# New time offsets for the steps of a two-layer graph attention kernel ordered by a timetable

## The chip, the cores and the metric

The kernel runs on one core of one Trainium2 chip. The metric is the device time of one execution in microseconds (us), the median of several. One profiled execution of the kernel is read as well: every time below that names an instruction comes from it, counted from the first instruction of the span. The engines are PE (TensorE, matmuls and transposes), DVE (VectorE), ACT (ScalarE), POOL (GpSimd) and SP (SyncE, which here only issues DMAs). "L1131" is line 1131 of the kernel before; the change makes the file 6 lines shorter, so the same line of the kernel after is L1125.

## What is computed

The input x has 16 batches of 1024 nodes with 256 features, adj is one 1024 x 1024 adjacency matrix for all batches. Two layers, both in fp32:

```python
# layer 0
h   = relu(layernorm(x))
r   = relu(h @ mlp1_w + mlp1_b)                   # 1024 x 512
o   = elu(gat(r, None, W_fc, a_fc)) + r           # dense attention, slope 0.2
r   = relu(o @ mlp2_w + mlp2_b)                   # 1024 x 256
o   = elu(gat(r, adj, W_hand, a_hand)) + r        # masked attention, slope 0.2
x   = x + relu(o)
# layer 1
h   = relu(layernorm(x)) @ W
x   = x + relu(softmax(where(adj == 0, -1e9, leaky_relu(f1 + f2, 0.01))) @ h)

def gat(inp, mask, W, a):
    h  = inp @ W
    e  = leaky_relu((h @ a[:F])[:, :, None] + (h @ a[F:])[:, None, :], slope)
    return elu(softmax(e, masked) @ h)
```

## The kernel before

**Stages of a batch.** A batch passes through these stages, each a small class whose methods are the steps; node tiles have 128 rows, the two halves h of a batch have four tiles each.

- Norm and BlockNorm: statistics (L571, L572), the root on POOL (L576, L577; for BlockNorm L613 to L616), centring on DVE (L581), then the turned copy: transposes nt on PE (L591) with a copy on ACT (L595), or, from batch 3 on, transposes in 32-blocks on DVE (L627) and moves by SP's DMAs (L637).
- Dense, the first attention. mlp1 (PE L805, ACT L808) gives resT; sums_of (DVE L819, L821, POOL L823, L825) forms sums of its rows, from which `step` (PE L834) makes the values h and adds them into hnat (ACT L856, DVE L866, L874). As this attention has no mask, its rows are sorted by their score instead of multiplied out: `highest` (PE extdps, DVE topd L911), `rank` for each of 8 tiles (DVE L926, L928, L930, L933), `scatter` of the rows to DRAM (POOL L940), `sign` (ACT L963) and `count` (DVE L969) for each node's place k, `read_sorted` (SP L984), running sums over the sorted rows (DVE L1012 to L1027), `write_table` (SP L1019) and `carry` (PE, ACT, SP L1041) into two tables in DRAM, a fine and a coarse one. `gather` (POOL L1051, indirect DMA) then fetches for every node tile a fine row, and adds the coarse row to it: 8 fine and 8 coarse gathers a batch, into four tiles got_b_h_i. `share` (DVE L1063 to L1066) makes the denominators den; `mean` is part on ACT (L1072) and hp on DVE (L1075). Batch 0 alone makes its first half by plain products instead: weights (L1095), od (PE L1103) and `product_mean` (hpd, L1110 to L1114).
- merge, four for each half: transposes hpT of the four hp on PE (L1121), three ACT operations (L1123 to L1125), then merge_end: e on DVE (L1131) and the add into resT on POOL (L1132). After it mlp2 (m2, PE L1139) with ACT's oT (L1142).
- Gnn0 and Gnn1, the two masked attentions: project (pa or pb on PE L669, copied by ACT L671), extremes (DVE L676, L677, PE extpsa or extpsb L546, DVE topa or topb L686), vectors, a row of the vector through DRAM (L551 to L554, L707), scale (ACT L716), the weights of eight tiles (atta, attb on DVE L722), product (oa, ob on PE L732), finish, combine, update and store.

PSUM has four buffers for mm (h, od, m, oa, ob), two for tr (nt, hpT, extps) and one for bc.

**What sets the order.** There is no loop order to read: every step is put into one table with a time, in units of about a microsecond, by `at`:

```python
def at(name, lo, hi, steps):
    for i, step in enumerate(steps):
        key = part + name
        moved = SHIFT.get(key, ())
        k = turn[key] = turn.get(key, -1) + 1
        when = lo + (hi - lo) * i / len(steps) + (moved[k] if k < len(moved) else 0.0)
        table.append((when, len(table), step))
```

`part` is "start " for the opening (batches 0 to 2 before the first period), "first " for batch 0's period, "mid " for the periods 1 to 12 and "end " for the last three. A period is 142 units in the table. Several batches are in flight in one period: in the period of batch b the masked attentions of b and b-1 run, the sorted sums, gathers, merges and mlp2 of b+1, and the norm, mlp1 and values of b+2 and b+3. SHIFT (L31 on) is a dict with an offset for each step of a name; steps beyond the tuple's length have offset 0. At the end the table is sorted by time, and the steps are issued in that order. The order on PE, DVE, ACT and SP is then fixed to it, and POOL's is fixed by added dependencies, except among scatters (L940):

```python
with tc.manual_schedule(engines={engine.PE, engine.DVE, engine.Activation, engine.SP}):
    for _, _, step in sorted(table, key=lambda entry: entry[:2]):
        step()
```

The times have no other effect: no engine waits for a time, only for its operands, for buffers, and for the instruction before it in its own order. So SHIFT decides who stands behind whom.

Of the kernel before, what the change touches and what calls it, by code (L numbers as in the profile page):

```python
# [31 lines left out]
    "end dense_begin1": (-5.56,),  # L32
    "end dense_begin2": (-5.2, -5.18,),
    "end dense_begin3": (-5.5,),
    "end dense_begin4": (0, -2.9, -8.1, -9.4, -12.6, -15.2, -16.2, -19.3,),
    "end dense_begin5": (-21.7, -21.7,),
    "end dense_begin6": (-28.9, -18.2, -16.02, -20.3, -24.3, -25.3,),
    "end dense_begin7": (-25.8,),
    "end dense_end1": (-12.1, -3.3,),
    "end dense_end2": (-12, -6.6, -10.6, -11.3, -2.6, -2.6, -2.6, -2.6,),  # L40
    "end dense_rows1": (-6.1, -4.2, -29.3, -23.4, -23.5, -14.8, -10.8, -13.4, -8.4, -6.6, -33.8,
        -30.8, -40.4, -34.9, -28.2, -31.9,),
    "end dense_rows2": (-13.4, -11.4, -1.5, -1.9, -10.7, -11.5, -21.9, -22.3, -13.6, -14.6, -8.3,
        -8.7, -6.5, 0, -24.5, -28, -23.8, -25.6, -18.6, -19.58,),
    "end dense_rows3": (-7.9, -2.4,),
    "end dense_rows4": (-24.8,),
    "end dense_sums10": (-42.6,),
    "end dense_sums11": (6.1,),
    "end dense_sums12": (-7.3,),
    "end dense_sums2": (-5.3, -3.9, -10.1, -10.2, -15.7, -13.2, -13.4, -12.6,),  # L50
    "end dense_sums3": (-8.7, -6,),
    "end dense_sums4": (-8.91, -10.158, -11.4, -12.648, -5.3, -5.3, -2.5, -3.4,),
    "end dense_sums7": (-3.2, -3.8, -4.6, -6, -6.8, -6.1, -7.7, -5.3,),
    "end dense_sums9": (-2.3,),
    "end early_gathers1": (-4.3, -4.29,),
    "end early_gathers2": (0, 0.002,),
    "end early_gathers3": (11.9, 19.3, 5, 13.2,),
    "end early_gathers4": (-8.55, -6.9, -1.7, -3.7, 9.2, 11.4, 4.7, 4.7,),
    "end first_mlp1": (-23.2, -18.7, -5.2, -8.6,),
    "end first_mlp2": (-52.8, -63.5, -84.1, -44.8,),  # L60
    "end masked_first1": (-16,),
    "end masked_first10": (-11.3, -10.91, -13.14, -13.74, -7.2, -8.1, -2.8, -3.4,),
    "end masked_first11": (-11.7, -11.1, -10.8, -11.45, -6.5, -7.2, -2.5, -3.1,),
    "end masked_first12": (-1.4, -1,),
    "end masked_first13": (-14.1, -13.6, -10.5, -11.76, -1, 1.3, 0, -1,),
    "end masked_first14": (-11.7, -8.6, -10.2, -11.95, 4.5, 4.5, 0, -0.5,),
    "end masked_first15": (-11.7,),
    "end masked_first16": (-0.3,),
    "end masked_first2": (-13,),
    "end masked_first3": (-14.3,),  # L70
    "end masked_first4": (-16.8,),
    "end masked_first5": (-18.4, -16.1, -16.5, -15.8, -13, -12.9, -16.3, -16,),
    "end masked_first6": (-24.6,),
    "end masked_first7": (-21.5, -16, -7.4, -22.8,),
    "end masked_first8": (-23.8, -6.8, -20.1, -18.4,),
    "end masked_first9": (-9.2, -10.06, -10.8, -10, -9.2, -9.8, -10.4, -10.9, -11.2, -11.63, -12.5,
        -10.8, -11.66, -11.6, -12, -12.7, -10.8, -10.8, -10.8, -10.8, -10.8, -10.8, -10.8, -10.8,
        -7.5, -6.9, -7, -6.9, -6, -5.3, -3.7, -3.7, -15.8, -10.7, -9.4, -7.5, -6.2, -4.3, -4.1,
        -2.2,),
    "end masked_second1": (-2.34, -3.204, -4.068, -4.932, -5.796, -6.6, -4.2, -4.2, -4.2, -4.2,  # L80
        -4.2, -4.2, -2, -2, -2, -2, -2, -2, -3.1, -2.34, -2.76, -3.18, -0.5, -0.9, -1.1, -1.1,
        -1.1, -1.1, -1.1, -1.1, -25.3, -24.3, -22.2, -18.2, -11, -10.97,),
    "end masked_second2": (-6.7, -6.7, -2.7, -2.7, -1.9, -1.9, -1, -1, -0.9, -0.9, -10.91,),
    "end masked_second3": (-7.2, -3.7, -2.81, -3.5, -1.5, -1.2, -0.7, -1.3,),
    "end masked_second4": (-4.6, -3.8, -3.7, -4.5,),
    "end masked_second5": (21.3, 31.4, 28.4, 30.2, 28.1, 19.5,),
    "end masked_second6": (0, 19.2,),
    "end merges1": (-5.9, -8.2, -2.29, -3.5, 0, -3, 3.3, 0.3,),
    "end merges2": (-3.2, -3, -3.96, -5.8, 3.5, 0.71, 2.7,),
    "end scatters1": (1.2, -0.6, -12.1, -8.7, -19.5, -21.3, -19.1, -24.8,),  # L90
    "end second_mlp1": (-8.9, 2.6, 1, 1.3,),
    "end second_mlp2": (-21.6, -13.8, -13.6, -22.6, -19.2, -20.4, -17.2, -22.2,),
    "end second_mlp3": (-17.9,),
    "end second_norm1": (-6.4, -5.3, -7.9, -8.2, -6, -7, -7.8, -8.6,),
    "end second_norm2": (-9.2,),
    "end second_norm3": (-9.3,),
    "end second_norm4": (-10.15,),
    "end second_norm5": (-10.3, -7.4, -7.5, -6.6, -7.5, -7.2, -5.41, -6.5,),
    "end second_norm6": (-12.3,),
    "end second_norm7": (-18.8,),  # L100
    "end second_norm8": (-32.2, -30.7, -31.2, 0, 0, 0, 0, -29.5,),
    "end turn_at1": (-8.8, -11.7, -12.1, -13.5, -1.46, -1.7, -2.1, -2.5,),
    "end turn_at2": (-8.1, -5.4, -7.8, -4.8, -2.6, -2.6, -2.6, -2.6,),
    "end weights a": (-18.1, -18.6, -19.1, -15.1, -10.2, -13, -9.7, -21.1, -8, -6.4, -11, -7.04,
        -7.85, -13.6, -10.9, -27.8, -9.7, -32.2, -10.2, -11.1, -11.4, -11.5, -15.1, -17.8, -11.6,
        -6.63, -6.7, -8.2, -6.9, -17.2, -6.7, -9.2, -11, -11.36, -10, -9.1, -11.3, -13.5, -4.7,
        -5.3,),
    "end weights b": (-9.3, -9.7, -9.5, -7.1, -8.6, -8.5, -4.1, -4.9, -5.8, -5.8, -5.8, -5.8, -5.8,
        -5.8, -5.8, -5.8, -8.8, -3.35, -2.8, -18.9, 0, -3, -12.5, -7.3, -1.5, -7.7, -2.7, 0, 0,
        -7.2, 0, 0, -7.4, 0, 0, 0, 1.8, 0, 0, 2, -25.9, -24.5, -22.9, -17.3, -10.4, -9.6, -12.8,  # L110
        -12.4,),
    "first dense_begin1": (-1.35,),
    "first dense_begin2": (-2,),
    "first dense_begin3": (-2.9,),
    "first dense_begin4": (-1.3, 2.4, 6.7, 0, 0, 0, -6.9, -11.7,),
    "first dense_begin5": (-20.3, -20.3,),
    "first dense_begin6": (-23.1, -28.8, -12.3, -26.6, -22.4, -21.7,),
    "first dense_end1": (-4.1, -4.3,),
    "first dense_end2": (-1.2, -4.1, -4.7, -3.8, 0.3, 0.3, 0.3, 0.3,),
    "first dense_rows1": (-13.9, -13.3, -20.1, -19.4, -21.8, -21.8, -17.1, -20.4, 0, -2.6, -25.3,  # L120
        -21.95, -28.5, -20.1, -23.2, -18,),
    "first dense_rows2": (-19.7, -20.3, -15.7, -12.5, -15.4, -20.8, -13.9, -13.9, -16.7, -18.5,
        -12.2, -13.43, 0, 0, -20.6, -15.8, -17.4, -11.7, -3.9, -12.2,),
    "first dense_rows3": (-19.01, -1.4,),
    "first dense_rows4": (-19.1,),
    "first first_mlp1": (-12.3, -10.8, -1.9, 15.9,),
    "first first_mlp2": (-2.8, -4.1, -22.3, -8.8,),
    "first first_norm3": (-38.92, -24.5, -24.1, -40.98, -32.7, -33.9, -31.3, -32,),
    "first first_norm4": (-24.9,),
    "first first_norm5": (-39.1, -39, -38.9, -37.7, -34.72, -45, -23.7, -22.7,),  # L130
    "first first_norm6": (-36.3, -36.2, -37.4, -36.4, -26.8, -26.8, -26.8, -26.8,),
    "first first_norm7": (-2.8, 0, 0, 6.3,),
    "first gathers1": (0, 6.1, 0, 3.75, -11.2, -6.4, -8.3,),
    "first gathers2": (1.4, 5.6, 0, 0, -4, 0, -20.8,),
    "first masked_first1": (-10.6,),
    "first masked_first10": (-9.64, -10.1, -9.2, -11.2, -2.8, -2, -3.8, -4.4,),
    "first masked_first11": (-9.6, -8.6, -7.44, -8.05, -1.4, -2, -4.99, -5.597,),
    "first masked_first13": (-9.6, -5.4, -11.4, -12.04, -5.36, -5.3, -8.5, -9.1,),
    "first masked_first14": (-6.4, -3.9, -10.2, -13, -5.3, -0.7, -8.1, -8.4,),
    "first masked_first15": (-13.3,),  # L140
    "first masked_first16": (-8.1,),
    "first masked_first4": (-12,),
    "first masked_first5": (-7.5, -7.5, -7.5, -7.5, -7.5, -7.5, -7.5, -7.5,),
    "first masked_first6": (-185.7,),
    "first masked_first8": (0, 0, 0, 13.1,),
    "first masked_first9": (-8.3, -9.1, -9.7, -10.3, -10.5, -11.2, -8.2, -8.9, -11.7, -11.7, -11.7,
        -11.7, -11.7, -11.7, -11.7, -11.7, -6.8, -6.8, -6.8, -6.8, -6.8, -6.8, -6.8, -6.8, -3.6,
        -3.6, -3.6, -3.6, -3.6, -3.6, -3.6, -3.6,),
    "first masked_second1": (-33, -31.5, -31.1, -23, -21.3, -17.9, -6.8, -5.8, -3.1, -2.7, 0, 0,
# [1848 lines left out]
```

## Time and profile before

| | |
|---|---|
| time, median of 3 runs | 2209.48 us (2209.32 to 2210.51) |
| the profiled execution | 2209.02 us, span 2207.3 us, mean granted clock 0.994 |
| busy | PE 98%, DVE 77%, ACT 61%, POOL 48% of the span |
| DMA | 373.45 MB, mean 169 GB/s; POOL's queue 29.5% of 16 engines' span, SP's and ACT's 33.4% |
| opening (before batch 0's masked attention gets going) | 0 to 240 us |
| a steady period | 131 us, from some 240 to 1875 us |
| ending | 1875 us to the end |

TensorE has one row of records for each matmul pass; an fp32 matmul that is not a transpose gives two records, a transpose one. "PEld" is the load of the stationary operand, which runs beside the matmuls. In a row of waits the columns are the waiting engine and line, what it waited for, and the total us, the number of times and the longest one. In a row of a timeline they are the start, the busy us, engine, line, operation, output <- inputs, shape, count, and in brackets the idle time before it and its releaser. In the table of stretches the granted clock (1.00 is full speed) follows the five engines' busy times, then the share of DMA.

### The profile page before, as it was taken

What the parts mean: (1) busy time and instruction counts of PE and PEld (TensorE: products, weight loads), DVE (VectorE), ACT (ScalarE), POOL (GpSimd) and SP (SyncE); (2) the same over time, 40 slices, a digit from 0 to 9 for tenths busy, and PEclk for the clock granted to TensorE, in tenths of its full rate; (3) what the DMA queues carried; (4) which work ended last, traced back from release to release, by engine and by line L of the source; (5) the groups of instructions that cost most, each with busy time, mean ns of one, the idle gap of its engine ahead of it and who ended that gap; (6) DMA issues with size and microseconds to landing.
All of it is one profiled execution on the core that took longest, in us unless ns stands there. A gap on an engine that the chain in (4) does not pass through costs nothing.

```text
span 2207.3 us, 31327 instructions
## 1 busy us (share of the span) xinstructions
PE 2162.5 (98%) x9498; PEld 1678.0 (76%) x9498; DVE 1689.1 (77%) x4801; ACT 1336.2 (61%) x2925; POOL 1064.5 (48%) x1344
## 2 busy tenths in 40 slices
PE   7989999999999999999999999999999999999998
PEld 5767778787887878778787877878788786877777
DVE  8867786787868779686877868778786876869755
ACT  5455755738566583855748476573856648375653
POOL 3343527365363645636365363745536364453520
PEclk9989999999999999999999999999999999999999
DMA  6367757666676766767676566766757675665700
GB/s 229 116 167 196 148 177 189 185 179 156 189 178 187 190 167 191 157 187 171 204 180 163 178 158 201 184 185 178 161 180 182 189 191 135 181 143 177 186 22 29
DMA packets 268754, 373.45 MB, mean 169 GB/s; under 512 B 124880, under 2 KB 180760, under 8 KB 264480
## 3 DMA queue, kind: packets, MB, share of 16 engines
q1 hardware_dynamic: 221968, 207.19, 33.4%
q0 software_dynamic: 45952, 163.99, 29.5%
q8 instruction: 78, 1.28, 0.3%
q14 instruction: 100, 0.82, 0.1%
q10 hardware_dynamic: 656, 0.17, 0.0%
HBM read 231.09 MB, written 126.56 MB: 162 GB/s over the span
## 4 chain that ended last, share of the span: by engine, by line
PE 85%; DVE 6%; POOL 5%; ACT 2%; issue 1%; DMA 0%; POOLq 0%; DVEq 0%; ACTq 0%
PE oa L732 19%; PE h L834 17%; PE ob L732 13%; PE m L805 10%; PE m L1139 9%; PE pb L669 5%; PE pa L669 5%; POOL got L1051 3%; PE hpT L1121 3%; PE nt L591 1%; PE on L1153 1%; DVE attb L722 1%; PE od L1103 1%; PE carry L1036 1%; POOL ea L761 1%
## 5 line engine op out<-in xcount | busy, mean ns | idle before, releaser
L732 PE MATMUL ob<-hmb,attb 128*128 128x257 f32 x2048 | 465.5, 381 | 1.9 <-DVE attb L722 1.1
L732 PE MATMUL oa<-hma,atta 128*128 128x258 f32 x2048 | 456.5, 381 | 1.6 <-DVE atta L722 1.3
L732 PEld LDWEIGHTS oa<-hma,atta 128*128 128x128 f32 x2048 | 386.6, 190 | 65.7 <-issue 7.7
L732 PEld LDWEIGHTS ob<-hmb,attb 128*128 128x128 f32 x2048 | 381.3, 190 | 65.0 <-issue 6.9
L722 DVE SCALAR_TENSOR_TENSOR atta<-rowsa,qwda,edge 128x256 f32<-128x256 f32 (+1 forms) x520 | 265.7, 542 | 61.9 <-DMA rowsa<-row_a 48.8
L760 POOL TENSOR_TENSOR posa<-posa,onat 128x256 f32<-128x256 f32 x118 | 94.8, 803 | 369.4 <-ACT posa L748 369.1
L1051 POOL DMA_INDIRECT got<-coarse,k x124 | 206.3, 1663 | 99.8 <-DMA got<-fine,k 40.2
L722 DVE SCALAR_TENSOR_TENSOR attb<-rowsb,qwdb,edge 128x256 f32<-128x256 f32 (+1 forms) x536 | 238.7, 480 | 17.6 <-PE ob L732 8.0
L805 PE MATMUL m<-hT,w_sb 128*128 128x512 f32 x512 | 237.8, 597 | 2.7 <-ACT rb L774 2.2
L1139 PE MATMUL m<-resT,w_sb 128*128 128x512 f32 x512 | 230.0, 597 | 0.0
L1132 POOL TENSOR_TENSOR resT<-resT,e 128x512 f32<-128x512 f32 x128 | 166.2, 1301 | 86.3 <-DVE e L1131 75.4
L747 ACT ACTIVATE ea<-oa,reca 128x256 f32<-128x256 f32 x128 | 60.5, 472 | 238.7 <-DVE reca L744 208.1
L774 ACT ACTIVATE rb<-ob,recb 128x256 f32<-128x256 f32 x128 | 58.0, 473 | 242.5 <-DVE recb L772 236.3
L940 POOL DMA_INDIRECT sorted<-hnat,place x128 | 126.6, 989 | 145.9 <-DVE place L933 89.5
L1139 PEld LDWEIGHTS m<-resT,w_sb 128*128 128x128 f32 x512 | 95.7, 192 | 102.3 <-issue 96.0
L805 PEld LDWEIGHTS m<-hT,w_sb 128*128 128x128 f32 x512 | 95.7, 191 | 88.9 <-issue 73.0
L1051 POOL DMA_INDIRECT got<-fine,k x124 | 134.8, 1087 | 57.6 <-issue 29.0
L963 ACT ACTIVATE junk<-r,fs 128x1024 int8<-128x1024 f32 x124 | 142.4, 1148 | 9.0 <-issue 3.8
L761 POOL TENSOR_TENSOR ea<-ea,posa 128x256 f32<-128x256 f32 x118 | 102.6, 869 | 79.5 <-ACT ea L754 42.4
L1131 DVE SCALAR_TENSOR_TENSOR e<-hpT,e 128x512 f32<-128x512 f32 x128 | 87.7, 686 | 68.1 <-ACT e L1125 50.5
L808 ACT ACTIVATE resT<-m,b_sb 128x512 f32<-128x512 f32 x128 | 87.7, 687 | 85.0 <-PE m L805 84.4
L834 PE MATMUL h<-wfc_sb,resT 128*128 128x257 f32 x512 | 129.3, 383 | 0.3 <-ACT hpd L1113 0.3
(211 smaller groups left out, 4260.9 us busy)
## 6 DMA issues: line engine op xcount, KB each, us to landing
xs<-sorted SPq DMA_DIRECT2D x32, 1028.0 KB
fine<-tt SPq DMA_DIRECT2D x32, 1026.0 KB
fine<-xs SPq DMA_DIRECT2D x32, 1026.0 KB
x<-in_x_dram SPq DMA_DIRECT2D x16, 1024.0 KB
xn<-in_x_dram SPq DMA_DIRECT2D x15, 1024.0 KB
out_dram<-x SPq DMA_DIRECT2D x28, 512.0 KB
hT<-xn SPq DMA_DIRECT2D x416, 32.0 KB
coarse<-carry SPq DMA_DIRECT2D x32, 256.5 KB
```

Of the source, the lines that this page charges most:

```text
L669: nc.tensor.matmul(ps[:, :2 + F], lhsT=hT[:, c, t * P:(t + 1) * P], rhs=self.w_sb[:, c, 0, :], start=(c == 0), stop=(c == FC - 1))
L722: nc.vector.scalar_tensor_tensor(a_t[:, :n * P], self.rows[:, i], self.qwd[:, 1, j:j + 1], edge[:, j, i], op0=OP.max, op1=OP.mult)
L732: nc.tensor.matmul(self.out[t][:, :F + self.ONES], lhsT=self.att[t0, j][:, (t - t0) * P:(t - t0 + 1) * P], rhs=self.hm[:, j, 2:2 + F + sel ...
L760: adder.tensor_add(pos, pos, o_nat[:, t, :])
L761: adder.tensor_add(e, e, pos)
L805: nc.tensor.matmul(ps, lhsT=w1_sb[:, kc, c * P:(c + 1) * P], rhs=piece(kc, h), start=(kc == 0), stop=(kc == FC - 1))
L834: nc.tensor.matmul(ps, lhsT=lhs[:, k, :], rhs=rhs[k], start=start and k == 0, stop=k == 1, skip_group_check=True)
L940: made = nc.gpsimd.indirect_dma_start(out=sorted_d[self.b % 2], out_offset=bass.IndirectOffsetOnAxis(ap=self.place[:, t:t + 1], axis=0), i ...
L963: nc.scalar.activation(junk, self.r2, AF.Sign, bias=self.fs[:, 0, t:t + 1], accum_out=self.signs[:, t:t + 1])
L1051: nc.gpsimd.indirect_dma_start(out=got[u // n][:, u % n, :], out_offset=None, in_=(coarse_d if coarse else fine_d)[self.b % 2][:, :], in_o ...
L1132: nc.gpsimd.tensor_add(dst, dst, e)
L1139: nc.tensor.matmul(ps, lhsT=w2_sb[:, kc, c * P:(c + 1) * P], rhs=self.resT[:, kc, h * HALF:(h + 1) * HALF], start=(kc == 0), stop=(kc == H ...
```

## The change

Only the dict SHIFT is replaced. It has 244 names before and 238 after; 239 names differ, in all four parts (66 of "mid ", 65 of "end ", 55 of "start ", 53 of "first "), 1581 offsets in all. No step, instruction, buffer or shape is added or removed; the order in which the same instructions are issued on PE, DVE, ACT, SP and POOL is another.

```diff
 SHIFT = {
...
-    "end second_mlp1": (-8.9, 2.6, 1, 1.3,),
-    "end second_mlp2": (-21.6, -13.8, -13.6, -22.6, -19.2, -20.4, -17.2, -22.2,),
-    "end second_norm1": (-6.4, -5.3, -7.9, -8.2, -6, -7, -7.8, -8.6,),
-    "end second_norm2": (-9.2,),
+    "end second_mlp1": (-12.9, 2.4, 1.5, -3.4,),
+    "end second_mlp2": (-21, -21, -21, -21, -21, -21, -21, -21,),
+    "end second_norm1": (-8.9, -7.2, -9.8, -6.22, -7, -7.9, -8.8, -9.65,),
+    "end second_norm2": (-10.1,),
...
-    "mid dense_end1": (-4.39, -5,),
-    "mid dense_end2": (0, -0.9, -1.2, 0.2, 3.1, 2, 2.4, 1,),
+    "mid dense_end2": (2.24, 1.9, 0.18, 0, 2.3, 2.3, 2.3, 2.3,),
-    "mid early_gathers1": (3, 3.5,),
-    "mid early_gathers2": (1.4, 2,),
-    "mid early_gathers3": (0, 20.6, -6.6,),
-    "mid early_gathers4": (12.5, 6.1, -7.3, 0, 7.6, 14.1, -3.4, 6.6,),
+    "mid early_gathers1": (8.1, 8.103,),
+    "mid early_gathers2": (2.3, 2.303,),
+    "mid early_gathers3": (0, 20.14, -6.8,),
+    "mid early_gathers4": (7.2, 14.4, 0, 0, 10.2, 10.7, -14.4, 5.9,),
+    "mid first_norm4": (-5.8,),
-    "mid merges1": (2.75, -2.3, 5, 3.5, 6.8, 4.5, 7.2, 6.6,),
-    "mid merges2": (6.3, 0, 4.5, 2.4, 4.5, 4.1, 7.5, 5.6,),
+    "mid merges1": (0, -6.2, 6.15, 3.18, 2.9, 4.2, 6.4, 5.3,),
+    "mid merges2": (6.1, -4.9, 6.9, 0.7, 5.1, 2.89, 6.5, 4.21,),
-    "mid second_mlp2": (-20.1, -17.9, -18.5, -14.7, -17, -16.4, -18.7, -20.7,),
+    "mid second_mlp2": (-19.4, -14.4, -20, -19.2, -17.3, -18.5, -17.6, -18.5,),
...
-    "start gathers1": (-1.19, -2.188, -3.2, -2.3,),
-    "start gathers2": (-2.1, 0, -5.8, 3.3,),
-    "start merges1": (-20.6, -21.8, -22.6, -24.5, 0, 2.7, 0.43, -10.4,),
-    "start merges2": (-16.4, -16.5, -17.6, -19.4, 7.8, 5.5, 4.8,),
+    "start gathers1": (-1.4, -1.4, -1.4, -1.4,),
+    "start gathers2": (-0.5, -0.5, -0.5, -0.5,),
+    "start merges1": (-20.3, -20.3, -20.3, -20.3, 0, 0, 0, -11.9,),
+    "start merges2": (-17.4, -19.4, -20.9, -21.3, 9.57, 7.3, 5,),
-    "start start28": (-6.4, -13.1, -13.8, -23.1,),
-    "start start32": (3.3, 0.7, -3.9, -6.9, -7.7, -10.4,),
-    "start start42": (-16.8, -26, -27.3, -21, -37.2, -30.8, -30.1, -39.8,),
+    "start start28": (-13.2, -20.8, -14.8, -21.6,),
+    "start start32": (0, 0, 0, -6.6, -18.8, 0, 0, -19.4,),
+    "start start42": (-19.6, -33.7, -37.8, -42.6, -39, -44.9, 0, -46.7,),
...
 }
```

The names: early_gathers1 to 3 are the fine gathers and early_gathers4 the coarse ones of a period, first_norm4 is BlockNorm's root (L613 to L616), dense_end1 and dense_end2 are share and mean, merges1 and merges2 the merges and their ends, second_mlp1 mlp2 and second_mlp2 project of Gnn0, second_norm1 and second_norm2 project and extremes of Gnn1; start28 is product_mean, start32 the ranks and start42 the signs of batch 1, gathers1 and gathers2 of "start " the fine and coarse gathers of batch 0's second half.

## The prediction

> **What bounds the kernel now.** I read, in this order, the busy times, TensorE's (PE's) waits, the stretches of the span, and the timelines of the places that lose time. The profiled execution took 2209.02 us, its span is 2207.3 us, the median of the three timed runs is 2209.48 us.
>
> ```profile
> PE 2162.5 (98%) x9498; PEld 1678.0 (76%) x9498; DVE 1689.1 (77%) x4801; ACT 1336.2 (61%) x2925; POOL 1064.5 (48%) x1344
> ...
> PEclk9989999999999999999999999999999999999999
> ```
>
> PE is the bound, and the change takes no matmul away. From start to start its records take 429 ns at 512 columns, 217 at 257 or 258, 109 at 128 in fp32 and 56 in bf16. Over the 9498 records this makes a floor of 2130.3 us for either order. The other 77.0 us of the span are 9.6 before the first matmul (it waits for x), about 7.3 after the last one starts, and 60 between matmuls. Where these 60 lie, the stretches show:
>
> ```profile
> 120.00:160.00 40.00, 31.57 (x126) 22.35 (x125) 24.89 (x73) 22.08 (x39) 22.82 (x29) 0.90 0.73 172
> 160.00:200.00 40.00, 37.92 (x152) 26.78 (x153) 28.41 (x67) 25.13 (x54) 7.58 (x9) 0.89 0.74 199
> ...
> 563.00:694.00 131.00, 131.00 (x576) 102.46 (x575) 102.27 (x289) 82.45 (x182) 67.20 (x85) 1.00 0.68 180
> 694.00:825.00 131.00, 130.66 (x574) 101.88 (x574) 100.60 (x289) 82.41 (x182) 67.98 (x85) 1.00 0.67 179
> ```
>
> The columns are the stretch, then PE, PEld, DVE, ACT and POOL busy, the granted clock and the DMA share. In the steady periods of 131 us PE has nothing to give: against the floor they lose 0.3 to 1.8 us each, 10 us from 240 to 1875. The opening 240 us lose 34 beside the first 9.6, half of that from 120 to 200; the ending from 1875 loses 15. So any gain must come from the two ends, and the middle can only be spoilt or left alone.
>
> **The change part by part.** Every instruction stays; their places on PE, DVE, ACT, SP and POOL move. I compare the two orders at the places that lose time.
>
> *First merge (138 to 172 us).* This is batch 0's two halves of merge (L1121 to L1132) and mlp2 (L1139). Before:
>
> ```profile
> PE hpT L1121 <- DVE e L1131: 7.6, 5, 4.1
> ...
> 142.91 2.51 DVE L930 SCALAR_TENSOR_TENSOR junk<-r,fs,after 128x128 uint8<-128x128 f32 x1
> ...
> 145.60 1.28 DVE L1131 SCALAR_TENSOR_TENSOR e<-hpT,e 128x512 f32<-128x512 f32 x2
> ...
> 146.43 1.09 PE L1121 MATMUL hpT<-ident,hpd 128*128 128x128 f32 x4 [4.12 <-DVE e L1131]
> 147.31 9.40 PE L1139 MATMUL m<-resT,w_sb 128*128 128x512 f32 x16
> 158.62 0.30 PE L1121 MATMUL hpT<-ident,got 128*128 128x128 f32 x1 [1.92 <-issue]
> ...
> 171.36 4.89 PE L1139 MATMUL m<-resT,w_sb 128*128 128x512 f32 x11
> ```
>
> The second L1131 stands behind a rank group (L926 to L933, 141.46 to 145.60), so PE's fourth hpT starts only at 146.43. The last coarse gather stands on POOL behind two more L1132 adds and starts at 149.0; its landing lets den (L1063) start at 155.5. ACT, in the way too, runs six signs (L963, 1.15 each) up to 157.0 before the first part (L1072). In the changed order the first two L1131 follow each other, the gather stands behind two adds in all, one sign lies among the e's and the rest are elsewhere. But both od sums now end together, and hpd_0_3 becomes late: the first hpT waits 0.7 us in place of 0.18. Step by step, with the durations above: od ends at 138.65, hpd_0_3 at 139.4, ACT's three ops (2.0 us) end at 141.9, L1131 (0.69) at 142.6; ACT's next three at 143.75, L1131 at 144.5, fourth hpT at 144.6 and not 146.4. POOL adds at 142.65 and 144.5 (1.27 each), then the gather at 146.0 (1.57); with the 4.9 us from its end to den before, den starts at 152.5. Part then starts at 153.65 and not at 157.0, and the chain from there to the last e is the old one, 3.3 us earlier. Among PE's work the changed order puts less in front of the second m2: it starts at 167.9 after its three pa and eight nt, with 129.5 us of pure PE work done; before it was 171.36 with 130.2. So 41.2 us of loss become 38.4: **a gain of 2.8 us**. Bounds: 1.0 if the rank group that now stands between the second and third L1131 meets the 2.5 us again, as POOL works beside it in the new place too; 5 if one of the half-clock spells (144.8 to 151.8 at 0.53, 158.5 to 168.9 at 0.52) goes with the idle time that precedes it.
>
> The long L930 is one of 120, whose median is 0.35 us. [...]
>
> *The wait at 55 us.* Here nt needs the buffer that DVE's topd (L911) still reads:
>
> ```profile
> 55.59 0.33 PE L591 MATMUL nt<-ident,hn 128*128 128x128 f32 x1 [2.00 <-DVE topd L911]
> ```
>
> The changed order puts two matmuls of h4 (four records, 0.87 us) ahead of it, so 1.1 us of the 2.0 remain: **gain 0.9**. Bounds: 0 if h4's own operand is late, 2.6 if the half-clock spell from 56.2 to 59.6 (3.4 us, 1.7 of loss) goes as well.
>
> *The end.* From 2006 on, pa (L669) of batches 14 and 15 stands directly behind the mlp2 (L1139) that feeds it through ACT's oT, and extpsb (L546) directly behind pb:
>
> ```profile
> PE pa L669 <- ACT oT L1142: 1.6, 3, 0.9
> ...
> PE extpsb L546 <- DVE extb L677: 1.5, 2, 0.8
> ...
> 2168.84 0.29 PE L546 MATMUL extpsb<-ident,extb 128*128 128x128 f32 x1 [0.76 <-DVE extb L677]
> ```
>
> The changed order leaves 3.0 us of other matmuls in front of those pa, and 0.87 us (two ob pairs) between the last pb and extpsb. That covers 0.85 + 0.20 + 2 x 0.76: **gain 2.6**, bounds 0.5 (extb is itself late on DVE) and 4 (on, extpsa, oa and ob lose another 1.5 there, by the timeline of 2117 to 2173).
>
> *Steady periods: the gathers.* The one part that can lose twelve times. On POOL the four small steps of the next batch's norm (L613 to L616) and a memset stood behind the coarse gathers of the first half (got_b_0_0); now they stand in front of its last two:
>
> ```profile
> 753.04 1.78 POOL L1051 DMA_INDIRECT got<-coarse,k  x1 [0.20 <-issue]
> 755.12 1.73 POOL L1051 DMA_INDIRECT got<-coarse,k  x1 [0.30 <-issue]
> 756.93 0.26 POOL L613 TENSOR_SCALAR shift<-mv 128x8 f32<-128x8 f32 x1
> ...
> 764.52 0.12 DVE L1063 TENSOR_TENSOR den<-got,qd 128x2 f32<-128x2 f32 x1
> ```
>
> From 756.93 to the next gather they take 2.8 us with the hand-over, and two posa/ea pairs move between the third and fourth fine gather, so the last of this half ends near 760.2 and not 756.85. Before, its landing (den at 764.5) came 7.7 us after POOL's end; the last gather of the period, with nothing in front of it, needed 4.5. So the difference is queueing: 16 gathers kept the DMA engines at 0.83 from 730 to 772. With 12 gathers ahead in both orders, the landing is then 760.2 + 4.5 = 764.7, or up to 0.6 later. PE wants hpT (L1121) 1.8 us earlier than before in its own order (723.2 against 725.0 us of pure work), while before it had 2.2 us to spare after the last hp (L1075). ACT's first part begins only at 766.6 behind its copies, 1.1 us after den, so a landing up to 765.6 is covered: **0**. Bounds: if the whole 3.3 us reaches the landing (767.8), 2.1 us per period are lost, 25 us in 12 periods; below nothing, 3 us won if the longer distances from mlp2 to pa (3.4 to 7.7, 0.9 to 2.6 us) empty the small waits of the periods. DVE's den for the second half now stands behind L1131 of the first, which takes DVE's 3.6 us wait at 773 off that merge.
>
> **Sum.** 2.8 + 0.9 + 2.6 + 0 = 6.3. 2209.02 - 6.3 = 2202.7 for a profiled execution, 0.46 more for a median: **2203 us**.
>
> **The rivals.** (a) *The gathers become the steady wait: slower.* One place: den L1063 waiting for got<-coarse, then PE's hpT behind hp. It decides once the landing is later than 765.6 on the scale above. For it: DVE already waits 48.0 us in 16 waits there, and PE has no other slack in these periods. Against: the queueing just described. Midway to the bound, 1.2 us in 12 periods, it costs 14: 2209.5 - 6.3 + 14 = 2217. (b) *The edges give little.* The rank group is held up again (1.0 at the merge), at 55 us h4 is late (0), the end gives 0.5: 2209.5 - 1.5 = 2208. For it: three of the gains lean on distances of a microsecond. (c) *The clock goes with the gaps.* The half-clock spells of 56 to 60, 145 to 152 and 158 to 169 us cost some 10 us in all; if most go, 8 more: 2195. [...]
>
> **How the numbers follow.** Forecast 46%, (a) 22%, (b) 22%, (c) 10%. The forecast's own range is 2200 to 2205. Down to (c) and up to (a) the range is 2196 to 2217. A measurement of this kernel tells about 0.2%, 4.4 us, from no change. Faster by more: forecast and (c), 56%; within: (b), 22%; slower: (a), 22%.
>
> **What would show it.** Right: the fourth hpT of the first merge starts near 144.6, den there near 152.5, extpsb waits for nothing, and the periods from 240 to 1875 stay at 131.0 us. Wrong: a new row of PE hpT waiting for DVE hp, with some ten occurrences, and DVE's wait at L1063 well above 48 us; or a first merge whose m2 still starts after 170.

## The result and the profile after

The changed kernel is slower. Its median is 2218.63 us (2213.2 to 2223.43, 10 runs) against 2209.40 for the kernel before in 10 runs: a ratio of 1.0039, with a 95% interval of 1.0026 to 1.0052. The profiled execution has a span of 2218.3 us, 11.0 more than before.

The page's busy times and the same stretches as before (stretch, PE, PEld, DVE, ACT and POOL busy, clock, DMA share, GB/s):

```profile
PE 2161.7 (97%) x9498; PEld 1674.9 (76%) x9498; DVE 1704.7 (77%) x4801; ACT 1326.6 (60%) x2925; POOL 1070.9 (48%) x1344
```

```profile
120.00:160.00 40.00, 30.28 (x120) 20.44 (x119) 23.95 (x73) 24.12 (x42) 25.50 (x27) 0.90 0.70 182
160.00:200.00 40.00, 40.00 (x164) 29.46 (x164) 29.50 (x75) 22.80 (x54) 6.92 (x8) 0.93 0.70 185
...
563.00:694.00 131.00, 130.02 (x571) 101.11 (x570) 102.31 (x288) 81.54 (x182) 67.98 (x85) 1.00 0.65 175
694.00:825.00 131.00, 128.45 (x564) 99.80 (x563) 100.16 (x281) 79.29 (x178) 67.96 (x85) 1.00 0.66 175
```

The second stretch shows the gain near the opening, PE now being busy through all of 160 to 200. The last one shows the loss: 128.45 us of PE in 131, where before it was 130.66. As a period no longer takes 131.0 us (from first fine gather to first fine gather it is 132.8 on average, before 131.2), stretches cut at equal times drift apart, so I compare by work instead. Between two marks of pure PE work (the sum of the matmul intervals in front) I take the time that passed less the work. In us:

| pure PE work | before | after | difference |
|---|---|---|---|
| 0 to 115 | 12.97 | 10.27 | -2.7 |
| 115 to 130 (first merge) | 18.25 | 16.92 | -1.3 |
| 130 to 250 | 3.33 | 0.86 | -2.5 |
| 250 to 1900 (steady) | 10.67 | 29.93 | +19.3 |
| 1900 to the last matmul | 14.70 | 12.20 | -2.5 |

The rest to 11.0 is the tail behind the last matmul, 0.7 longer. So the two ends gain 9.0 us, and the steady periods, where there was nothing to win, lose 19.3. What PE waits for there, between 300 and 1900 us (engine and line, what it waited for, total us, times, longest), after:

```profile
PE pb L663 <- ACT hmb L665: 8.1, 7, 1.7
PE oa L726 <- DVE atta L716: 3.2, 5, 1.5
PE pb L663 <- ACT part L1066: 2.7, 3, 1.0
PE ob L726 <- DVE attb L716: 2.5, 2, 1.6
```

and before:

```profile
PE m L805 <- ACT rb L774: 2.2, 6, 0.5
PE ob L732 <- DVE attb L722: 0.5, 2, 0.3
PE ob L732 <- ACT rb L774: 0.2, 1, 0.2
```

The wait of pb is new and comes in ten of the twelve periods. By the same measure as in the table (time from start to start of PE's records, less the usual time of each) the matmuls of pb lose 15.8 us between the marks of 250 and 1900, where they lost 0.6 before; that is most of the 19.3. One of these waits, followed back through the timelines of POOL, DVE, ACT and PE (start, us, engine, line, what; idle before and releaser in brackets):

```profile
748.69 1.79 POOL L1045 DMA_INDIRECT got<-coarse,k  x1 [0.20 <-issue]
...
751.21 1.67 POOL L609 TENSOR_TENSOR rstd<-rstd,power 128x8 f32<-128x8 f32 x1
...
755.31 1.59 POOL L1045 DMA_INDIRECT got<-coarse,k  x1 [0.16 <-issue]
...
764.32 0.16 DVE L1057 TENSOR_TENSOR den<-got,qd 128x2 f32<-128x2 f32 x1 [2.09 <-DMA got<-coarse,k]
...
765.12 0.72 ACT L1066 ACTIVATE part<-got,den 128x513 f32<-128x513 f32 x1 [1.30 <-DVE den L1060]
...
766.63 0.64 ACT L665 COPY hmb<-pb 128x258 f32<-128x258 f32 x2
...
767.04 1.14 PE L663 MATMUL pb<-wl_sb,hT 128*128 128x258 f32 x4 [1.02 <-ACT hmb L665]
```

The root's four steps (L609 is the long one) stand between the gathers, the last of the first half ends at 756.9, den waits 2.09 us for its landing, ACT stands 1.30 us at the first part, and the copies that empty PSUM for the next pb stand behind that part. PE waits for a buffer whose matmuls ended near 765.2 and whose copy came at 766.63, 1.4 us later.

### The profile page after: what moved, and what is told of

Read it like the earlier page. It is cut to its first block, busy times and chain, and to the rows that moved or that the text cites. A ratio compares the mean times of both kernels' runs of the same rounds, so it can differ in the third digit from the quotient of the medians.

```text
span 2218.3 us, 31328 instructions
## 1 busy us (share of the span) xinstructions
PE 2161.7 (97%) x9498; PEld 1674.9 (76%) x9498; DVE 1704.7 (77%) x4801; ACT 1326.6 (60%) x2925; POOL 1070.9 (48%) x1344
## 5 line engine op out<-in xcount | busy, mean ns | idle before, releaser
L726 PE MATMUL oa<-hma,atta 128*128 128x258 f32 x2048 | 463.6, 382 | 4.2 <-DVE atta L716 3.9
L726 PEld LDWEIGHTS oa<-hma,atta 128*128 128x128 f32 x2048 | 384.4, 190 | 76.2 <-DVE atta L716 11.8
L754 POOL TENSOR_TENSOR posa<-posa,onat 128x256 f32<-128x256 f32 x118 | 108.0, 916 | 365.8 <-ACT posa L742 362.3
L716 DVE SCALAR_TENSOR_TENSOR attb<-rowsb,qwdb,edge 128x256 f32<-128x256 f32 (+1 forms) x536 | 253.4, 508 | 14.9 <-PE ob L726 13.6
L716 DVE SCALAR_TENSOR_TENSOR atta<-rowsa,qwda,edge 128x256 f32<-128x256 f32 (+1 forms) x520 | 252.4, 524 | 13.0 <-DMA rowsa<-row_a 6.7
L1126 POOL TENSOR_TENSOR resT<-resT,e 128x512 f32<-128x512 f32 x128 | 172.5, 1348 | 129.4 <-DVE e L1125 111.7
L663 PE MATMUL pb<-wl_sb,hT 128*128 128x258 f32 x512 | 129.8, 384 | 11.3 <-ACT hmb L665 8.1
L755 POOL TENSOR_TENSOR ea<-ea,posa 128x256 f32<-128x256 f32 x118 | 93.7, 794 | 78.4 <-ACT ea L748 68.5
```

The source lines that it names most:

```text
L663: nc.tensor.matmul(ps[:, :2 + F], lhsT=hT[:, c, t * P:(t + 1) * P], rhs=self.w_sb[:, c, 0, :], start=(c == 0), stop=(c == FC - 1))
L716: nc.vector.scalar_tensor_tensor(a_t[:, :n * P], self.rows[:, i], self.qwd[:, 1, j:j + 1], edge[:, j, i], op0=OP.max, op1=OP.mult)
L726: nc.tensor.matmul(self.out[t][:, :F + self.ONES], lhsT=self.att[t0, j][:, (t - t0) * P:(t - t0 + 1) * P], rhs=self.hm[:, j, 2:2 + F + sel ...
L754: adder.tensor_add(pos, pos, o_nat[:, t, :])
L755: adder.tensor_add(e, e, pos)
L1126: nc.gpsimd.tensor_add(dst, dst, e)
```

## The experiments

All ratios are to the kernel before on the same chip in the same session. Offsets in the short diffs are those of SHIFT. "12th gather" is the time from the start of a period's first fine gather to the end of its twelfth on POOL, "den" that to the second L1063 operation of the first half; both are means over 12 steady periods.

| kernel | median us | ratio (95%) | 12th gather | den |
|---|---|---|---|---|
| before | 2207.8 to 2209.4 | 1 | 24.0 | 32.2 |
| changed | 2218.6 | 1.0039 (1.0026 to 1.0052) | 26.2 | 33.7 |
| old_middle | 2198.3 | 0.9953 (0.9938 to 0.9967) | 24.2 | 32.4 |
| new_middle | 2232.9 | 1.0111 (1.0096 to 1.0127) | 26.3 | 34.0 |
| root_early | 2236.6 | 1.0137 (1.0120 to 1.0153) | 23.0 | 31.3 |
| root_idle | 2199.4 | 0.9966 (0.9955 to 0.9977) | 23.4 | 31.8 |
| stats_only | 2213.2 | 1.0022 (1.0013 to 1.0032) | 26.2 | 33.4 |
| root_doubled | 2210.5 | 1.0016 (1.0007 to 1.0024) | 26.3 | 33.7 |
| gathers_first | 2243.2 | 1.0150 (1.0129 to 1.0171) | 23.5 | 35.4 |
| parts_late | 2217.1 | 1.0043 (1.0029 to 1.0058) | 26.2 | 33.8 |
| parts_hpT_late | 2209.0 | 1.0005 (0.9994 to 1.0016) | 26.3 | 33.7 |
| root_parts_hpT | 2205.7 | 0.9993 (0.9983 to 1.0004) | 23.6 | 32.1 |
| old_sums | 2251.4 | 1.0207 (1.0184 to 1.0231) | 26.1 | 33.1 |
| old_root_idle | 2253.5 | 1.0207 (1.0193 to 1.0221) | 24.1 | 32.2 |

**Which stretch loses.** Both sets of offsets are kept, and each step gets a time by either. A cut at 114 and one at 1850 of the table choose the order:

```diff
-            table.append((when, len(table), step))
+            table.append((new, len(table), step, old))
...
+    parts = sorted([e for e in table if e[0] < 114.0], key=lambda e: (e[0], e[1]))
+    rest = [e for e in table if not e[0] < 114.0]
+    parts += sorted([e for e in rest if e[3] < 1850.0], key=lambda e: (e[3], e[1]))
+    rest = [e for e in rest if not e[3] < 1850.0]
+    parts += sorted(rest, key=lambda e: (e[0], e[1]))
```

old_middle (new ends, old middle):

> Steps in the changed order up to time 114 of the table (about 250 us), then all remaining steps in the old order up to 1850, then the rest in the changed order. By pure PE work the changed kernel lost 6.6 us less than the old one up to 250 us, about 17 more from 250 to 1900 and 2.5 less after that. Theory A (the steady periods alone lose, the two ends keep their gains): 2209.4 - 6.6 - 2.5 = about 2200, ratio 0.996, periods back at 131.0 us, no wait of pb. Theory B (the old and new pieces depend on each other, the gains at the start are bought by what comes later): 2206 or more, with new waits at the seams.

Measured 2198.3, ratio 0.9953: theory A. The new ends keep their gains without the new middle, and between 300 and 1900 us PE waits as it did before:

```profile
PE m L1087 <- ACT rb L1056: 1.6, 4, 0.6
```

new_middle, the reverse:

> The reverse: the old order up to time 114, the changed one up to 1850, the old one for the rest. Theory A: 2209.4 + 17 = about 2226, with the waits of pb for ACT's copies, oa and ob as in the changed kernel. Theory B: under 2220.

2232.9, and the waits of pb are there (13.6 us in 11). It lies above theory A's 2226, and the seam itself costs: 11.0 us of loss between 250 and 381 us of work, where the two parent kernels have 1.6 and 0.8. A cut between two orders needn't be free.

**What in the middle loses: the root on POOL.** In root_early the root goes ahead of the fine gathers:

```diff
-    "mid first_norm3": (-58.2, -57.9, 0, -59.6, -59.8, -61.58, -61.7, -61.8,),
-    "mid first_norm4": (-5.8,),
+    "mid first_norm3": (-58.2, -57.9, -59.5, -59.6, -59.8, -61.58, -61.7, -61.8,),
+    "mid first_norm4": (-23.3,),
```

> The changed kernel, with BlockNorm's root (four small POOL steps, some 2.6 us) moved in the steady periods from between the coarse gathers to ahead of the fine ones, and one of its eight statistics on DVE moved with it. Theory A1 (the gathers' landing follows POOL's issue, so what stands between them delays den, ACT's part and with it the copies of pb): the last coarse gather of the first half ends some 2.3 us earlier, den some 2 us earlier, the waits of pb fall from 10.8 us to under 3, the time to about 2208 to 2211. Theory A2 (the landing is set by the DMA engines' throughput, not by POOL's order): den does not move by more than 0.6 us, the waits of pb stay, time 2218 as before.

Half right, and the time went the other way. den moved by 2.4 us for 3.2 us of earlier issue, so the landing does follow POOL's issue (A1), and the waits of pb fell from 10.8 us to 0.6. But 2236.6, by a new wait:

```profile
PE ob L726 <- DVE attb L716: 26.6, 11, 3.1
...
DVE x L759 <- POOL ea L755: 59.8, 17, 5.4
```

Two pairs of posa and ea stand between the fine gathers. The root ahead of them delays them, DVE waits at the update of x (L759) with attb queued behind it, and PE waits for attb. Theory A1 had priced only the gathers behind the moved steps, not the adds among them. root_idle puts the root where POOL stands idle 16 us, ahead of the first posa:

```diff
-    "mid first_norm4": (-5.8,),
+    "mid first_norm4": (-56.0,),
```

> The changed kernel, with BlockNorm's root (and one statistics step with it) moved in the steady periods to where POOL idles 16 us before its first posa of the period, so ahead of neither the fine gathers nor posa and ea. Theory A1 (landing follows POOL's issue, and the new wait of ob in the kernel with the root ahead of the fine gathers came from posa and ea behind that root): the 12th gather ends 23 to 24 us after the first fine one begins (26.3 in the changed kernel), den of the first half 31 to 32 us after it (33.7), the waits of pb fall from 10.8 us to under 2, and ob does not rise above the 2.5 us of the changed kernel: 2206 to 2210. Rival (earlier gathers cause the wait of ob by themselves, by their traffic): ob at 15 us or more again, 2220 or more.

2199.4, ratio 0.9966, below what A1 expected. Of PE's waits between 300 and 1900 us one row is left,

```profile
PE oa L726 <- DVE atta L716: 1.1, 3, 0.5
```

and at the place shown above PE runs through pb without a gap, while the last wait of that half's gathers on DVE is gone:

```profile
757.53 0.12 DVE L1057 TENSOR_TENSOR den<-got,qd 128x2 f32<-128x2 f32 x1
...
759.60 0.73 ACT L1066 ACTIVATE part<-got,den 128x513 f32<-128x513 f32 x1
...
760.00 2.78 PE L663 MATMUL pb<-wl_sb,hT 128*128 128x258 f32 x12
```

den now stands ready 1 us before ACT comes to the part. The rival (earlier gathers cause ob's wait by their traffic) falls: the gathers are as early as in root_early, and ob waits for nothing. stats_only is the control for the statistics step that had to move along (the third offset of first_norm3):

> Control: the changed kernel with only the one statistics step moved, the root where the changed kernel has it. All theories: as the changed kernel, 2215 to 2221.

2213.2, ratio 1.0022, so a little below; its interval overlaps that of the changed kernel, and whether that step is worth something by itself is open. The root's move is worth the step from 1.0022 to 0.9966, some 12 us.

**Delay of the gathers, or ACT's wait for the root's result?** The root had two followers in the changed kernel, as ACT's hn also stood 45.6 us waiting for shift. root_doubled keeps the root in the idle time and adds four equal steps on a spare tile at the changed kernel's place:

```diff
+        def again(self):
+            nc.gpsimd.tensor_scalar(spare, power, -1.0, None, op0=OP.mult)
+            nc.gpsimd.tensor_scalar_add(spare, spare, EPS)
+            nc.gpsimd.tensor_tensor(spare, spare, power, OP.pow)
+            nc.gpsimd.tensor_tensor(spare, spare, spare, OP.mult)
...
+        if part == "mid ":
+            at("again", t0 + 60.5, t0 + 60.5, [n.again])
```

> The kernel with the root in POOL's idle time (2199.4), and with four more POOL steps of the same kinds and sizes, on a spare tile that nobody reads, where the changed kernel has its root, between the coarse gathers. They delay the gathers as the root did, but ACT's hn needn't wait for them. Theory G (the root's harm is the delay of the gathers): the 12th gather ends 26 us after the first fine one again, den moves back to 33 to 34 us, pb waits 8 us or more, 2214 to 2220. Theory H (its harm is ACT's hn, which stood 45.6 us waiting for shift with the other ACT work behind it): 2197 to 2203.

2210.5, ratio 1.0016, 11 of the 12 us, and den is back at 33.7. The waits are back as well:

```profile
PE pb L670 <- ACT hmb L672: 4.7, 5, 1.7
PE pb L670 <- ACT part L1073: 3.7, 6, 0.8
PE oa L733 <- DVE atta L723: 1.9, 3, 1.4
```

The time is below the 2214 to 2220 expected, since that was reckoned from the changed kernel and not from stats_only; beside the control it fits theory G. PE's losses at pb between 250 and 1900 us of work say the same: 15.8 us in the changed kernel, 10.8 in stats_only, 0.6 in root_idle, 11.8 in root_doubled. gathers_first takes the other part: the last two coarse gathers of the half go ahead of the root, which is then late for ACT.

```diff
-    "mid early_gathers4": (7.2, 14.4, 0, 0, 10.2, 10.7, -14.4, 5.9,),
+    "mid early_gathers4": (6.9, 5.1, 0, 0, 10.2, 10.7, -14.4, 5.9,),
```

> The changed kernel (with the one statistics step ahead) where the two last coarse gathers of the first half stand ahead of the root, as in the old order: the gathers are early, shift is 3.7 us later than in the changed kernel. Theory G: pb's waits for parts go. But hn then waits 3 to 4 us a period longer at the head of ACT's queue, so theory H, and G in part, have PE wait for copies behind it (nt, pb): 2215 or more if that has no slack, 2200 to 2206 if it has.

2243.2. The 12th gather is early (23.5) and yet den is late (35.4), and the waits are of another kind:

```profile
PE pb L663 <- ACT resT L802: 23.7, 12, 2.7
...
764.39 0.60 ACT L614 ACTIVATE hn<-xn,shift,rstd 128x256 f32<-128x256 f32 x1 [6.65 <-POOL shift L610]
```

ACT stands 6.65 us at the first hn with mlp1's copies behind it. den is late for the same reason and not for its rows: DVE, ahead of den, waits for ACT's resT, 118.2 us in 12 waits between 300 and 1900 us where it was 73.4 in the changed kernel. So hn's wait has no slack left either, and in the changed order the root can't simply go back behind these gathers. The two constraints squeeze the root from both sides, and of the places tried only POOL's idle time before the gathers serves both.

**Is it ACT's order, or PE's?** parts_late moves the first two parts behind the copy of pb_6, parts_hpT_late moves hpT_1 behind three more matmuls as well, and root_parts_hpT joins both to root_idle:

```diff
-    "mid dense_end2": (2.24, 1.9, 0.18, 0, 2.3, 2.3, 2.3, 2.3,),
-    "mid merges1": (0, -6.2, 6.15, 3.18, 2.9, 4.2, 6.4, 5.3,),
+    "mid dense_end2": (2.24, 1.9, 0.55, 0.225, 2.3, 2.3, 2.3, 2.3,),
+    "mid merges1": (0, -4.2, 6.15, 3.18, 2.9, 4.2, 6.4, 5.3,),
```

> The changed kernel, with the first two parts (ACT) of the first half moved behind the copy of pb_6 in the steady periods, and the two hp on DVE behind them. Theory A1 (the gathers land too late for where PE wants hpT): the wait of pb goes, and a wait of hpT for hp of 0.6 to 1.1 us a period takes its place, so the time changes by less than 6 us, 2213 to 2219. Rival A3 (only ACT's order is at fault: parts that wait for den stand ahead of copies that could run): the waits of pb, 10.8 us, go with nothing in their place: 2207 to 2209.

2217.1: A1. The wait only changes its name,

```profile
PE hpT L1115 <- DVE hp L1069: 11.1, 15, 0.8
```

> The changed kernel with the first two parts behind the copy of pb_6, as before, and the first merge of each period (hpT_1) two units of the table later, behind three more matmuls of h, 2.7 us of PE work. Theory A1 (supply later, demand earlier: hpT stood 1.8 us earlier in PE's work): the 11.1 us of hpT waiting for hp fall to under 2 and nothing takes their place: 2205 to 2209. Rival (the merge being late moves the wait to e, m2 or h): 2213 or more, with a wait of m or of hpT on DVE's e.

2209.0, at the upper edge of A1: the waits fall to 3.1 us in all, which leaves the middle with some 1.3 us of loss a period, spread over small waits, most of them of h and extpsb. Asking later gives back about half of what the middle had lost.

> The changed kernel with all of these: the root in POOL's idle time, the parts behind the copy of pb_6, hpT_1 later. Theory A1: no wait of pb, hpT on hp, and about 6 us of oa and ob left in the steady periods, so 2204 to 2208; not better than the old middle with the new ends (2198), because the sorted rows still land late and the atta and attb stay behind them.

2205.7, in the expected range, and worse than root_idle alone by 0.0027. The moved parts and hpT have a price of their own: between 250 and 1900 us of work h loses 6.3 us where it loses 1.0 in root_idle, and extpsb 2.8 where it loses 0.2, nearly as much as in parts_hpT_late (7.1 and 3.4).

**Misses.** old_sums gives the changed kernel the old offsets of the eight names dense_sums of "mid " that differ, so that the running sums stand behind three more atta.

> The changed kernel with the old offsets for the sorted sums of the steady periods (signs, sum weights, running sums): the first running sums stand behind three more atta on DVE. Theory C (the waits of oa come from DVE standing at the first running sum, whose rows land late, with atta behind it): the 3.2 us of oa waiting for atta go to under 0.5, while the tables, and with them the fine gathers, come up to 1.9 us later, so that the waits of pb and ob grow: 2216 to 2230. Rival (atta are late for their own operands): oa keeps its 3 us.

2251.4, and theory C as put falls: oa's waits grew to 8.1 us in 12, ob's to 10.3. The edit moved signs, count and sums together, so it doesn't tell which of them did it. That oa's waits of the changed kernel fall to 1.1 us in root_idle, with the sums where they were, shows that the sums' place isn't their cause by itself. old_root_idle gives the old kernel root_idle's offsets of first_norm3 and first_norm4.

> The old kernel with the root in POOL's idle time and the statistics of the changed kernel for it. In the old kernel the root stood behind the first half's gathers and ahead of the second half's. Theory G: the first half's gathers don't move, PE loses 0.3 to 1.8 us a period there, so there is little to win: 2205 to 2209. Rival (the root among gathers costs as such, wherever it stands): 2200 or less.

2253.5. The first half's gathers don't move, as theory G says (24.1 and 32.2), but this was no clean test. All eight offsets of the statistics came along on DVE, five of them moved by 58 to 62 units, and PE waits 13.5 us in 12 for atta and 14.0 in 11 for ACT's rb. Which of them did it is open. Offsets that serve one order wrecked the other.

## Why the prediction was wrong, point by point

- **The bound.** Right: PE, nothing to win in the middle, and "can only be spoilt or left alone". It was spoilt: the periods did not stay at 131.0 us.
- **First merge.** The mechanism was right and the size half: 1.3 for 2.8. The two L1131 run one after the other, the fourth hpT waits 1.25 us for e and not 4.12, den starts 7.8 us after it (7.9 predicted, 9.1 before). What I left out stands in the second half: before, two matmuls of pa lay between its second and third hpT; the change puts them behind all four, so the third now waits 2.5 us. The row names no releaser; DVE's e of the first, whose buffer it needs, ends at 157.77:

```profile
157.82 1.12 PE L1115 MATMUL hpT<-ident,got 128*128 128x128 f32 x4 [2.52 <-issue]
...
166.66 5.74 PE L1133 MATMUL m<-resT,w_sb 128*128 128x512 f32 x13
```

  The L930 that I feared would meet POOL again took 0.35 us in all three rank groups there. That is luck and no test of what an add beside it does: none of the three ran beside one, as the adds ended 0.02 and 0.01 us ahead of two of them. The median of 0.35 us said little either. Of all 128 L930 of the kernel before, 124 ran beside no POOL operation or beside DMA issues alone; of the other four two took 0.35 us (beside the root's L576, and beside the last 0.09 us of an add) and two took longer: 0.76 beside a sum (L823) and 2.51 beside a whole add (L1132).
- **The wait at 55 us.** 1.7 us less between 30 and 60 us of work, against 0.9 predicted: the wait of nt for topd went from 2.0 to 0.2 and the clock of 56 to 60 stayed at 1.00 where it was 0.57 (the upper bound's condition); 1.2 came back as a new wait of mask_ps and 0.9 as one of h for POOL's s. PE was busy 2.76 of the 3 us ahead, before it was 1.00. The longest gap in these 3 us was 2.0 us before and 0.24 after; what brings the clock down is not shown by that.
- **The opening elsewhere.** Not foreseen: 1.2 us less from 60 to 115 and 2.5 from 130 to 250 us of work, small waits that I hadn't compared one by one.
- **The end.** 2.5 for 2.6: extpsb waits 0.3 us where it waited 1.5, pa no longer waits. The mechanism is as forecast, and the size is right in part by luck: new waits (extpsa 1.5 us where it was 0.5, rowspsb 0.9) and smaller ones that I hadn't priced (oa 0.6 where it was 1.6) lie beside it.
- **The gathers: the step that failed.** I let the queue in front of the DMA engines swallow POOL's delay, with 4.5 us from the end of the 12th gather to den in place of 7.7: "764.7, or up to 0.6 later". In the changed kernel it is 7.4 us (756.90 to 764.32 above). The 12th gather came 2.2 us later after the first, not 3.3, and 1.5 of these 2.2 reached den. Counted from the first fine gather as in the period of the prediction (there at 732.97, here at 730.54), den came at 766.75, past the 765.6 that I had named as the limit, and ACT stood idle 1.30 us for it. And I looked for the waiter at hpT behind hp. ACT's queue has another: in the changed order two parts stand ahead of the copies of pb_6 and pb_4, so den is needed when ACT gets there, not when PE wants hpT. I had seen these parts in ACT's order and not asked who waits behind them. The term priced at 0, with bounds of 3 us won and 25 lost, measured 19.3 lost, of which the root's place gives back 11 to 12. For the rest the one statistics step is the candidate, and it isn't shown (1.0039 to 1.0022, intervals that overlap).
- **The rivals.** (a) was the right one: the place (den waiting for got<-coarse) and, at 2217, nearly the time, though with 14 lost in the middle for 19 and 6.3 won at the ends for 9.0. Its signs did not come: hpT waits 0.3 us for hp in the whole run, and DVE's wait at L1063 fell from 48.0 to 26.3 us. The waiter on PE was pb. The range ended at its 2217 instead of its upper part, so 2218.6 lies outside. (c) came in part: 1.00 for 0.57 at 56 to 60, and at the merge 0.70 and 0.97 in 140.0 to 144.8 and 144.8 to 151.8, where it was 1.00 and 0.53. What the clock gave of the merge's 1.3 isn't separated.

## What to carry to other kernels

When a step moves on an engine, ask what else that engine's queue holds for a bottleneck that has no slack: here ACT stood 1.30 us at a part for its den, and the copy behind it, which reads no den, came 1.4 us after the matmuls of its pb had ended. Four small steps put back between the gathers made the 12th gather 2.9 us later and den 1.9 (root_doubled beside root_idle: 26.3 for 23.4, 33.7 for 31.8), so put such steps where the issuing engine idles and the step's own reader still gets its result in time, and check the adds that stand there as well. Judge a new order by parts: here two good ends and a bad middle made one slower kernel, and the new ends with the old middle (2198.3) or the changed kernel with the root's four small steps and one statistics step moved (2199.4) beat both.

## What the runs showed of the hardware

That the DMA engines are busy 0.83 of the time while a period's gathers run (730 to 772 us before, 728 to 770 after; 0.63 to 0.69 over whole periods) didn't mean that landings are set by their throughput here. In the steady periods den starts 7.8 to 8.6 us after the end of the 12th gather in the kernel before and 6.7 to 8.2 in the changed kernel; by the means of the table it is 8.3 in root_early, whose gathers end 1 us earlier than before. A gather issued sooner landed sooner by most of the difference: 23.0 (root_early), 24.0 (before) and 26.2 us of issue (changed) gave den at 31.3, 32.2 and 33.7.
